# A graph layer on one core: silu by one ScalarE instruction, for two octs at a time, and another order in front

## The chip, the core and the metric

The kernel runs on one core of a Trainium2 chip. A core has TensorE (PE), VectorE (DVE), ScalarE (ACT), GpSimd (POOL) and SyncE (SP), each with its own queue of instructions, which it takes strictly in order; they meet at semaphores. The metric is the device time in microseconds. The kernel before takes 825.34 us, the median of three runs (822.86 to 827.72).

## The reference

12,500 nodes with 128 features and 400,000 edges, sorted by destination. Cut to what matters:

```python
rbf = exp(-(dist[:, None] - centers) ** 2 / (2 * width ** 2))      # 50 centers
cut = 0.5 * (cos(pi * dist / 10) + 1) * (dist <= 10)
W   = (silu(rbf @ fw1 + fb1) @ fw2 + fb2) * cut[:, None]
agg = segment_sum((h[src] @ pw + pb) * W, dst)
y   = h + (silu(agg @ mw1 + mb1) @ mw2 + mb2)
out = layernorm(h + y)
```

`dist` is `edge_weight`. Edges longer than the cutoff add nothing, and the kernel drops them: 141 quads of 512 edges are left to compute.

## The kernel before, in words

**Chunks and packing.** The edges are read in 7 chunks. `pack(c)` (a Python generator that emits some instructions at each step) squeezes the dropped edges out of a chunk on VectorE, scatters the lines that are left to `packed` in DRAM, reads them back (`pair`), and stores the lengths to `near_d`. It then makes `srci` (the source indices, for GpSimd's gathers), `base` and `dl` (where a message goes) and `cut`. `cut` needs a sine on ScalarE. Turning a row of these into places on partitions costs a transpose on TensorE each (L527) and a copy on VectorE (L529). Chunk 0 holds quads 0 to 6, chunk 1 quads 7 to 25, chunk 2 starts at quad 26.

**Projection.** `proj = h @ pw + pb` is computed for all nodes, in 25 tiles of up to four blocks of 128 rows: load, `turn` (transposes, and a copy to `xT` on ScalarE), `project` (matmuls, a copy to `hp` on ScalarE, a store by SP).

**Gathers.** `fetch(q)` is four indirect DMAs on GpSimd (L643), 128 rows each, into one of 8 quad buffers; from quad 24 on there are only four, because `own` takes the other four for messages and one-hot matrices. Quads 0 to 7 are gathered from `x` itself, so that they need not wait for `proj`; `multiply(q)` applies `pw` to them afterwards. From quad 8 on the gathers read `proj`.

**Filter.** Two quads make an oct. For each oct: `radials` has SP load the lengths, broadcast (`d`); `basis` is a square and an exp on ScalarE (L678, L679); `first` is the product with `fw1` into `ph`, of which there is one buffer (L688). `tanh` on ScalarE (L694) and `silu` on VectorE (L701) make s = (1 + tanh(ph / 2)) * ph, which is twice silu; `fw2_h`, half of `fw2` (L1035), makes up for it. `second(q)` is the product with that for one quad (L710, L713).

**Message and sum.** `message(q)` multiplies the filter with the gathered rows on VectorE (L720). `place(q)` makes the one-hot matrix times `cut` (L729), `sum_up(q)` multiplies the two on TensorE (L745), and `add` adds the result into `aggT` (L768). `nodes` does the second network and the layer norm for rows that are finished, among the quads; `finish` does the last ones.

**Order.** The order is written out by hand (`manual_schedule`): each engine gets its instructions in the order in which the Python code emits them. `clock`, `pool`, `tensor`, `awake` and `there_at` are the author's estimates of time; they decide only where pieces of `pack`, gathers and multiplications are emitted. `pack_until(us)` emits packing up to such a time. `ahead(k)` starts the filter in the last four tiles. After the projection `pack_until(math.inf)` emits all that is left of chunks 0 and 1 before message 0. The main loop then does, for quad q: packing, gathers for later quads, tanh, first and basis for later octs (every second quad), message q, second(q + 2), sum, place(q + 1), adds, silu.

**Tables.** ScalarE holds one set of activation functions at a time. Where the next function isn't in it, the built program has a table load, which stands in the profile as ACT_TABLE_LOAD with the line of that function.

Of the kernel before, what the change touches and what calls it, by code (L numbers as in the profile page):

```python
# [10 lines left out]
F32 = mybir.dt.float32  # L11
BF16 = mybir.dt.bfloat16
I32 = mybir.dt.int32
AF = mybir.ActivationFunctionType
OP = mybir.AluOpType
# [4 lines left out]
P = 128  # L20
# [6 lines left out]
QE = QT * P  # L27
# [11 lines left out]
NQ = QB[-1]  # L39
# [18 lines left out]
def kernel(  # L58
# [37 lines left out]
    nc = tc.nc  # L96
# [44 lines left out]
    def load_rows(c):  # L141

        raw[c] = []
        for name, ap, dt in (("r_d", edge_weight, I32), ("r_dst", dst, I32), ("r_src", src, I32)):
            t = work.tile([P, R_MAX], dt, name=name, bufs=2)[:, :ROWS[c]]
            v = ap[P * sum(ROWS[:c]):P * sum(ROWS[:c + 1])].rearrange("(r l) -> r l", r=P)
            nc.sync.dma_start(t, v if ap is not edge_weight else v.bitcast(I32))
            raw[c].append(t)
# [211 lines left out]
    def pack(c):  # L360
# [110 lines left out]
        else:  # L471
            awake[0] = 0.0
            if c > 1:
# [4 lines left out]
        pair = work.tile([64, 3, 512], I32, name="pair", bufs=1)  # L478
        dma.dma_start(pair[:np_], packed[:, p0 * 512:(p0 + np_) * 512]
                          .rearrange("s (p w) -> p s w", w=512))  # L480
        awake[c] = max(awake[c], clock[0]) + (7.5 if c == 1 else 3.5)
        yield 0

        def paired(dt, name):
# [116 lines left out]
    def project(t0):  # L601
        r = rows(t0)
        b = bank()
        h = b.rearrange("p (k f) -> p k f", k=4)
        rows_times(h, xT_of.pop(t0), pw_sb, bias_b["pb"], r)
        hp = work.tile([P, 4, H], F32, name="hp", bufs=3)
        for a, c, m in alike(r):
            nc.scalar.copy(hp[:m, a:a + c], h[:m, a:a + c])
        free.append(b)
        node_dma(t0, hp, proj, True)  # L610
# [37 lines left out]
    def quads(o):  # L648

        return [q for q in (2 * o, 2 * o + 1) if q < NQ]  # L650
# [20 lines left out]
    def chunk_of(q):  # L671
        return max(c for c in range(NC_) if QB[c] <= q)

    def basis(o):
        d, n = d_of.pop(o)
        u = n * 64
        rbf = work.tile([P, QE], F32, name="rbf")
        nc.scalar.activation(rbf[:u], d[:u], AF.Square, bias=rbf_bias[:u], scale=rbf_scale[:u])  # L678
        nc.scalar.activation(rbf[:u], rbf[:u], AF.Exp, scale=-1.0 / (2.0 * width * width))  # L679
        rbf_of[o] = rbf, n  # L680

    def first(o):

        rbf, n = rbf_of.pop(o)
        ph = ps.tile([P, 2, QE], F32, name="ph", bufs=1)
        for h in range(n):
            p0 = h * 64
            nc.tensor.matmul(ph[:, h, :], w1_sb[p0:p0 + KR], rbf[p0:p0 + KR], start=True, stop=True)  # L688
        ph_of[o] = ph, n

    def tanh(o):
        ph, n = ph_of[o]
        t = work.tile([P, 2, QE], F32, name="t", bufs=1)
        nc.scalar.activation(t[:, :n], ph[:, :n], AF.Tanh, scale=0.5)  # L694
        t_of[o] = t

    def silu(o):

        ph, n = ph_of.pop(o)
        s = work.tile([P, 2, QE], F32, name="s")  # L700
        nc.vector.scalar_tensor_tensor(s[:, :n], t_of.pop(o)[:, :n], 1.0, ph[:, :n],  # L701
                                       op0=OP.add, op1=OP.mult)
        for h in range(n):
            s_of[2 * o + h] = s[:, h]

    def second(q):

        s = s_of.pop(q)
        pu = bank()
        nc.tensor.matmul(pu, ones_b[:, :P], bias_b["fb2"].rearrange("k j f -> k (j f)"), start=True,  # L710
                         stop=False)
        for j in range(QT):
            nc.tensor.matmul(pu[:, j * H:(j + 1) * H], s[:, j * P:(j + 1) * P], fw2_h,  # L713
                             start=False, stop=(j == QT - 1))
        pu_of[q] = pu

# [7 lines left out]
    def place(q):  # L724

        hot = own(q, "hot", 1)
        for j in range(QT):
            at = 2 * q + j // 2, slice(j % 2, j % 2 + 1)
            nc.vector.tensor_scalar(hot[:, j, :], iota_n[:, :W], dl[:, at[0], at[1]],  # L729
                                    cut[:, at[0], at[1]], op0=OP.is_equal, op1=OP.mult)  # L730
        hot_of[q] = hot

    def windows(q):

        return 1 if chunk_of(q) < WIDE_C else 2
# [224 lines left out]
    def pack_until(us, among=2):  # L960

        while clock[0] < us and todo and todo[0] < among:
            have = [c for c in todo[:2] if c < among]
            c = next((c for c in have if awake[c] <= clock[0]), None)
            if c is None:
                clock[0] = min([us] + [awake[c] for c in have])
            else:
                go_on(c)
# [19 lines left out]

    def ahead(k):

        if k < 3:
            basis(k)
        if 0 < k:
            if k < 3:
                first(k - 1)
            if 1 < k:
                tanh(k - 2)
                silu(k - 2)
                clock[0] += 1.2

    for k, t0 in enumerate(tiles):
        if k + AHEAD_X < len(tiles):
            load_x(tiles[k + AHEAD_X])
        if loads and k >= 4 and k % 2 == 0:
            nc.sync.dma_start(*loads.pop(0))
        if k == 12:
            clear_packed(1, nc.sync)
        if k in (16, 19, 22):
            if k > 16:
                take_off()  # L1010
                clock[0] += 0.3
            take_off = part_of("fb2", fb2_f, (k - 16) // 3, False)
        if k == 23:
            load_rows(2)
        project(t0)
        clear(1, CLEARED)
        if k + 2 < len(tiles):
            turn(tiles[k + 2])
        tensor += 1.95
        pack_until(tensor)  # L1020
        fetches(tensor, FROM_X)
        while times[0] < fetched[0] and there_at[times[0]] <= tensor:
            multiply(times[0])
            times[0] += 1
            tensor += 1.9
            pack_until(tensor)
            fetches(tensor, FROM_X)
        if k in (17, 20, 23):
            radials((k - 14) // 3)
        if k >= len(tiles) - 4:  # L1030
            ahead(k - len(tiles) + 4)
    pack_until(math.inf)
    assert not loads and todo[0] == 2
    fw2_h = keep.tile([H, H], F32, name="fw2_h")
    nc.vector.tensor_scalar(fw2_h, fw2_sb, 0.5, None, op0=OP.mult)  # L1035
    fetches(clock[0], FROM_X)
    for q in (0, 1):
        second(q)
    first(2)
    place(0)  # L1040


    total, counted = None, []
    for q in range(NQ):
        while todo and todo[0] <= chunk_of(min(q + 3, NQ - 1)):
            go_on(todo[0])
        nodes(q)
        most[0] = min(NQ, max(min(q + GOT, sum(LATER)), q + LATER[1]))
        fetches(clock[0], most[0])
        fetches(math.inf, min(NQ, q + AHEAD + 1))  # L1050
        assert fetched[0] > min(NQ - 1, q + AHEAD)
        multiplies(q + 2)
        if q >= CLEAR_Q:
            clear()
        if loads_later and q >= 8:
            nc.sync.dma_start(*loads_later.pop(0))
        radials(q // 2 + 5)
        if q % 2 and q + 3 < NQ:
            tanh((q + 3) // 2)
        if q % 2 == 0 and 0 < q < NQ - 4:  # L1060
            first(q // 2 + 2)
        if q % 2 and q + 5 < NQ:
            basis((q + 5) // 2)
        msg = message(q)
        if q + 2 < NQ:
            second(q + 2)
        sum_up(q, msg)
        now = range(added(q), added(q + 1))
        for k in now:
            base_of(k, (0,))  # L1070
        if q + 1 < NQ:
            place(q + 1)
        for k in now:
            base_of(k, (1,))
            add(k)
        if q % 2 and q + 3 < NQ:
            silu((q + 3) // 2)
        clock[0] = max(clock[0], there_at[q])
        summed[q] = clock[0] + 0.7
        clock[0] += (3.1 if q % 2 else 1.9) + 0.3 * (windows(q) - 1)  # L1080
        if q == 1:
            clear_packed(2, nc.sync)
        if q + 1 < NQ:
            pack_until(max(there_at[q + 1], clock[0] + PACK_US), NC_)
        if NODES - 8 <= q < NODES - 2:
            part_of(*(("mb1", mb1_f) if q < NODES - 5 else ("mb2", mb2_f)), (q - NODES + 8) % 3)
        elif q == NODES - 2:
            late["mw2"] = mw2_h = keep.tile([H, H], F32, name="mw2_h")
            nc.vector.tensor_scalar(mw2_h, mw2_sb, 0.5, None, op0=OP.mult)
        if not todo and not counted:  # L1090
            counted.append(q)
            count()
        elif counted and total is None:
            total = nc.values_load(bad_i[0:1, 0:1], min_val=0, max_val=2 * E)
# [6 lines left out]
    with tc.If(total > 0):  # L1101
        nc.vector.memset(aggT, 0.0)
        def again(e0, seen):
# [21 lines left out]
            radial(-1, [edge_weight[ds(e0, QE)].rearrange("(o e) -> o e", o=1)])  # L1125
            basis(-1)
            first(-1)
            tanh(-1)
            silu(-1)
            second(-2)  # L1130
            u = own(0, "msg", 0)
# [51 lines left out]
```

## Time and profile before

| | |
|---|---|
| median of 3 runs | 825.34 us |
| profiled execution | 823.01 us |
| its span | 821.2 us |
| PE, DVE, ACT, POOL busy | 599.3, 662.6, 301.3, 571.8 us |
| tanh (L694) | 71 x 1015 ns |
| product for silu (L701) | 71 x 1207 ns |
| square and exp (L678, L679) | 71 x 806 and 71 x 630 ns |
| table loads | 15 x 1283 ns |
| gathers from `proj` | 532 x 990 ns, from 96.0 us on |
| mean granted clock | 0.856 |

Busy times are those of the span. In a row of a group of instructions come the line, the engine, the operation, what is written from what, and the count; then busy time, the mean time of one in ns, and the idle time just before them with what ended most of it ("issue": nothing that the profile shows). In a timeline row come the start, the duration and the same names, and in brackets the idle time before it and what it waited for. Idle time of an engine that sets nothing costs nothing. In such rows `fw_h` and `fw_sb` stand for `fw2_h` and `fw2_sb`.

### The profile page before, as it was taken

To read this page: it belongs to the slowest core of one execution; us is meant where nothing else is said; L and a number is where in the kernel's file an instruction comes from. 1 tells how busy PE (TensorE), PEld (TensorE's weight loads), DVE (VectorE), ACT (ScalarE), POOL (GpSimd) and SP (SyncE) were. 2 spreads that over 40 slices of the span, in tenths; PEclk is the share of its full clock that TensorE was granted. 3 is DMA by queue.
4 is the path that set the end of the run, shared out by engine and by line. 5 is a ranking of instruction groups with operands and counts; after the bars stand their busy time and mean duration, and the time that the engine had idled before them with its cause. 6 is when DMAs were issued, how large, how long until landed. Compare 5 with 4: busy or idle time off the path is not lost.

```text
span 821.2 us, 11643 instructions
## 1 busy us (share of the span) xinstructions
PE 599.3 (73%) x3492; PEld 463.6 (56%) x3492; DVE 662.6 (81%) x1857; ACT 301.3 (37%) x475; POOL 571.8 (70%) x585
## 2 busy tenths in 40 slices
PE   6874688777787676677768787878776786788661
PEld 6763566556565464565546466655554664666541
DVE  8852699999999788888998879888676766877774
ACT  7556343324334251223332333534331622251511
POOL 1474477777777777777777777777777777777740
PEclk9997699989978888687887887998999888999976
DMA  8984623243234223322242333543532543362221
GB/s 234 304 223 142 176 84 94 62 124 108 83 101 109 70 76 99 92 89 86 60 136 79 91 99 90 137 125 91 155 93 65 159 116 88 94 158 70 84 83 48
DMA packets 88189, 91.86 MB, mean 112 GB/s; under 512 B 13864, under 2 KB 67832, under 8 KB 88120
## 3 DMA queue, kind: packets, MB, share of 16 engines
q1 hardware_dynamic: 69320, 52.77, 21.9%
q0 software_dynamic: 18544, 38.17, 17.2%
q8 instruction: 29, 0.48, 0.2%
q14 instruction: 40, 0.33, 0.1%
q10 hardware_dynamic: 256, 0.11, 0.1%
HBM read 75.29 MB, written 15.71 MB: 111 GB/s over the span
## 4 chain that ended last, share of the span: by engine, by line
DVE 31%; DMA 21%; POOL 18%; issue 15%; PE 9%; DVEq 3%; ACT 2%; SPq 0%; POOLq 0%; ACTq 0%
DMA quad<-proj,srci 19%; POOL quad L643 18%; DVE hot L729 5%; DVE s L701 4%; DVE quad L729 3%; DVE aggT L768 3%; PE bank L277 3%; DVE msg L720 2%; DVEq L754 2%; PE sums L745 2%; DVE quad L720 1%; DMA x<-in_x_dram 1%; DVE st L808 1%; PE bank L713 1%; DVE r_d L438 1%
## 5 line engine op out<-in xcount | busy, mean ns | idle before, releaser
L643 POOL DMA_INDIRECT quad<-proj,srci x532 | 526.9, 990 | 171.7 <-issue 119.1
L713 PEld LDWEIGHTS bank<-fw_h,s 128*128 128x128 f32 x1128 | 177.9, 225 | 15.3 <-issue 7.5
L713 PE MATMUL bank<-fw_h,s 128*128 128x128 f32 x1128 | 177.5, 309 | 0.0
L688 PE MATMUL ph<-rbf,w_sb 51*128 51x512 f32 x282 | 98.0, 768 | 76.6 <-DVE s L701 60.1
L745 PE MATMUL sums<-hot,msg 128*128 128x128 f32 x696 | 111.3, 311 | 39.8 <-DVE msg L720 39.6
L694 ACT ACTIVATE t<-ph 128x1024 f32<-128x1024 f32 (+1 forms) x71 | 72.1, 1015 | 177.0 <-PE ph L688 173.4
L745 PEld LDWEIGHTS sums<-hot,msg 128*128 128x128 f32 x696 | 99.8, 221 | 47.1 <-DVE msg L720 46.7
L729 DVE TENSOR_SCALAR hot<-iota_n,dl,cut 128x128 f32<-128x128 f32 x348 | 97.7, 355 | 3.6 <-issue 1.0
L701 DVE SCALAR_TENSOR_TENSOR s<-t,ph 128x1024 f32<-128x1024 f32 (+1 forms) x71 | 85.7, 1207 | 16.9 <-ACT t L694 16.8
L720 DVE TENSOR_TENSOR msg<-bank,quad 128x512 f32<-128x512 f32 x87 | 59.4, 683 | 44.6 <-DMA quad<-proj,srci 39.9
L745 PE MATMUL sums<-quad,quad 128*128 128x128 f32 x432 | 68.4, 309 | 32.2 <-DVE quad L720 32.1
L745 PEld LDWEIGHTS sums<-quad,quad 128*128 128x128 f32 x432 | 61.6, 220 | 36.7 <-DVE quad L720 36.5
L688 PEld LDWEIGHTS ph<-rbf,w_sb 51*128 51x128 f32 x282 | 26.3, 214 | 98.2 <-issue 70.0
L768 DVE TENSOR_TENSOR aggT<-aggT,sums 128x128 f32 x212 | 60.6, 286 | 18.2 <-PE sums L745 7.2
L782 ACT ACTIVATE zt<-bank 128x512 f32<-128x512 f32 (+1 forms) x25 | 14.6, 587 | 165.2 <-PE bank L780 165.2
L710 PE MATMUL bank<-fb_b,ones_b 96*128 96x512 bf16 x141 | 61.6, 437 | 4.1 <-DVE msg L720 1.6
L729 DVE TENSOR_SCALAR quad<-iota_n,dl,cut 128x128 f32<-128x128 f32 x216 | 60.8, 350 | 2.3 <-issue 0.5
L720 DVE TENSOR_TENSOR quad<-bank,quad 128x512 f32<-128x512 f32 x54 | 37.1, 686 | 28.3 <-DMA quad<-proj,srci 28.1
L678 ACT ACTIVATE rbf<-d,rbf_bias,rbf_scale 128x512 f32<-128x512 f32 (+1 forms) x71 | 57.2, 806 | 5.1 <-DMA d<-near_d 5.0
L710 PEld LDWEIGHTS <-ones_b 96*128 96x128 bf16 x141 | 14.5, 103 | 68.7 <-issue 68.0
L847 ACT ACTIVATE x<-x,by,rs 128x128 f32<-128x128 f32 x91 | 36.9, 480 | 39.6 <-DVE by L817 39.6
L643 POOL DMA_INDIRECT quad<-in_x_dram,srci x32 | 33.1, 1033 | 20.2 <-DVE srci L529 10.0
(172 smaller groups left out, 746.2 us busy)
## 6 DMA issues: line engine op xcount, KB each, us to landing
d<-near_d SPq DMA_DIRECT2D x141, 128.0 KB
x<-in_x_dram SPq DMA_DIRECT2D x48, 256.0 KB
quad<-proj,srci POOLq DMA_INDIRECT x532
proj<-hp SPq DMA_DIRECT2D x24, 256.0 KB
out_dram<-x SPq DMA_DIRECT2D x24, 256.0 KB
packed<-zero_i SPq DMA_DIRECT2D x6, 188.0 KB
pair<-packed SPq DMA_DIRECT2D x3, 264.0 KB
r_d<-in_edge_weight_dram SPq DMA_DIRECT2D x3, 256.0 KB
```

Of the source, the lines that this page charges most:

```text
L643: nc.gpsimd.indirect_dma_start(out=got[:, j, :], out_offset=None, in_=proj if table is None else table, in_offset=bass.IndirectOffsetOnAxi ...
L678: nc.scalar.activation(rbf[:u], d[:u], AF.Square, bias=rbf_bias[:u], scale=rbf_scale[:u])
L688: nc.tensor.matmul(ph[:, h, :], w1_sb[p0:p0 + KR], rbf[p0:p0 + KR], start=True, stop=True)
L694: nc.scalar.activation(t[:, :n], ph[:, :n], AF.Tanh, scale=0.5)
L701: nc.vector.scalar_tensor_tensor(s[:, :n], t_of.pop(o)[:, :n], 1.0, ph[:, :n], op0=OP.add, op1=OP.mult)
L710: nc.tensor.matmul(pu, ones_b[:, :P], bias_b["fb2"].rearrange("k j f -> k (j f)"), start=True, stop=False)
L713: nc.tensor.matmul(pu[:, j * H:(j + 1) * H], s[:, j * P:(j + 1) * P], fw2_h, start=False, stop=(j == QT - 1))
L720: nc.vector.tensor_mul(msg, pu.rearrange("p (j f) -> p j f", j=QT), got_of.pop(q))
L729: nc.vector.tensor_scalar(hot[:, j, :], iota_n[:, :W], dl[:, at[0], at[1]], cut[:, at[0], at[1]], op0=OP.is_equal, op1=OP.mult)
L745: nc.tensor.matmul(pa[:, k * W:(k + 1) * W], msg[:, j, :], hot[:, j, :], start=(j % n == 0), stop=(j % n == n - 1))
L768: nc.vector.tensor_add(to, to, pa[:, k * W:(k + 1) * W])
L847: nc.scalar.activation(y[:m, k, :], y[:m, k, :], AF.Identity, bias=by[:m, k:k + 1], scale=rs[:m, k:k + 1])
```

## The change

`tanh` and the product become one activation, `Silu`, which reads `ph` and writes s; s has three buffers, and `fw2` is used as it is. In the main loop the filter goes by groups of four quads, that is two octs: at the fourth quad of a group the bases of two octs are computed, at the first and second quad of the next group `first` and `silu` of one oct each. `second` comes before `first` in each step.

In front: `ahead` does two bases and two silus; only quads 0 to 3 are multiplied among the tiles; chunk 2 is read at tile 17 instead of 23, and its packing may start among the tiles; after the projection only as much of chunk 1 is emitted as its indices need, and the rest of it comes among the first quads. The estimates of time differ too (a tile 2.25, a multiplication 2.1, a quad 2.2), and one clearing of `packed` moves from quad 1 to quad 0.

```diff
-        awake[c] = max(awake[c], clock[0]) + (7.5 if c == 1 else 3.5)
+        awake[c] = max(awake[c], clock[0]) + (10.5 if c == 1 else 3.5)
...
     def basis(o):
+        if o not in d_of:
+            for q in quads(o):
+                while chunk_of(q) not in stored:
+                    go_on(todo[0])
+            radials(o + 1)
...
-    def tanh(o):
-        ph, n = ph_of[o]
-        t = work.tile([P, 2, QE], F32, name="t", bufs=1)
-        nc.scalar.activation(t[:, :n], ph[:, :n], AF.Tanh, scale=0.5)
-        t_of[o] = t
-
     def silu(o):
-
         ph, n = ph_of.pop(o)
-        s = work.tile([P, 2, QE], F32, name="s")
-        nc.vector.scalar_tensor_tensor(s[:, :n], t_of.pop(o)[:, :n], 1.0, ph[:, :n],
-                                       op0=OP.add, op1=OP.mult)
+        s = work.tile([P, 2, QE], F32, name="s", bufs=3)
+        nc.scalar.activation(s[:, :n], ph[:, :n], AF.Silu)
...
-        if k < 3:
+        if k < 2:
             basis(k)
-        if 0 < k:
-            if k < 3:
-                first(k - 1)
-            if 1 < k:
-                tanh(k - 2)
-                silu(k - 2)
-                clock[0] += 1.2
+        if k > 1:
+            first(k - 2)
+            silu(k - 2)
...
-        if k == 23:
+        if k == 17:
             load_rows(2)
+            awake[2] = tensor + 10.0
...
-        tensor += 1.95
-        pack_until(tensor)
+        tensor += 2.25
+        among = 2 if k < 17 else 3
+        pack_until(tensor, among)
         fetches(tensor, FROM_X)
-        while times[0] < fetched[0] and there_at[times[0]] <= tensor:
+        while times[0] < min(fetched[0], 4) and there_at[times[0]] <= tensor:
...
-    pack_until(math.inf)
-    assert not loads and todo[0] == 2
-    fw2_h = keep.tile([H, H], F32, name="fw2_h")
-    nc.vector.tensor_scalar(fw2_h, fw2_sb, 0.5, None, op0=OP.mult)
+    while known[0] < QB[2]:
+        go_on(todo[0])
+    assert not loads
...
     for q in (0, 1):
         second(q)
-    first(2)
+    basis(2)
+    basis(3)
     place(0)
+
+    def octs(q):
+
+        return q // 4 * 2 + 2 + q % 4
...
-        if q % 2 and q + 3 < NQ:
-            tanh((q + 3) // 2)
-        if q % 2 == 0 and 0 < q < NQ - 4:
-            first(q // 2 + 2)
-        if q % 2 and q + 5 < NQ:
-            basis((q + 5) // 2)
         msg = message(q)
         if q + 2 < NQ:
             second(q + 2)
+        if q % 4 < 2 and 2 * octs(q) < NQ:
+            first(octs(q))
+            silu(octs(q))
+        if q % 4 == 3:
+            for o in (q // 4 * 2 + 4, q // 4 * 2 + 5):
+                if 2 * o < NQ:
+                    basis(o)
...
-        if q % 2 and q + 3 < NQ:
-            silu((q + 3) // 2)
...
-        clock[0] += (3.1 if q % 2 else 1.9) + 0.3 * (windows(q) - 1)
-        if q == 1:
+        clock[0] += 2.2 + 0.3 * (windows(q) - 1)
+        if q == 0:
             clear_packed(2, nc.sync)
```

More of the change, by code (lines that the diff above doesn't have):

```diff
@@ L712, in second @@
         for j in range(QT):
-            nc.tensor.matmul(pu[:, j * H:(j + 1) * H], s[:, j * P:(j + 1) * P], fw2_h,
+            nc.tensor.matmul(pu[:, j * H:(j + 1) * H], s[:, j * P:(j + 1) * P], fw2_sb,
                              start=False, stop=(j == QT - 1))
@@ L1018 @@
             turn(tiles[k + 2])
-        tensor += 1.95
-        pack_until(tensor)
+        tensor += 2.25
+        among = 2 if k < 17 else 3
+        pack_until(tensor, among)
         fetches(tensor, FROM_X)
-        while times[0] < fetched[0] and there_at[times[0]] <= tensor:
+        while times[0] < min(fetched[0], 4) and there_at[times[0]] <= tensor:
             multiply(times[0])
             times[0] += 1
-            tensor += 1.9
-            pack_until(tensor)
+            tensor += 2.1
+            pack_until(tensor, among)
             fetches(tensor, FROM_X)
@@ L1127, in again @@
             first(-1)
-            tanh(-1)
             silu(-1)
```

## The prediction, made before the changed kernel ran

> **What bounds the kernel now.** I read the table of engines first and the idle time of the busiest engines second. VectorE has the most busy time, yet the row that matters is GpSimd's gathers:
>
> ```profile
> span 821.2 us, 11643 instructions
> ...
> PE 599.3 (73%) x3492; PEld 463.6 (56%) x3492; DVE 662.6 (81%) x1857; ACT 301.3 (37%) x475; POOL 571.8 (70%) x585
> ...
> L643 POOL DMA_INDIRECT quad<-proj,srci x532 | 526.9, 990 | 171.7 <-issue 119.1
> ```
>
> 532 gathers cost 990 ns each, and in front of each one lie about 0.30 us of issue: 532 x 0.30 = 160 of the 171.7 us idle. So of the 171.7 us only some 12 are real waits. Four gathers make a quad: about 5.2 us a quad, 695.4 us from the first gather out of `proj` (96.03) to the end of the last (791.41). In this stretch GpSimd never stands still. The span is three pieces: 96.0 us of front, 695.4 us of gathers, 29.8 us of tail.
>
> The table by stage says the same: GpSimd runs 46 to 48 instructions in every 60 us, whether VectorE is nearly full (130 to 240 us) or not (600 to 660):
>
> ```profile
> 130.00:240.00 110.00, 81.62 (x492) 65.43 (x491) 106.93 (x272) 36.45 (x48) 84.43 (x84) 0.89 0.31 91
> 240.00:300.00 60.00, 43.01 (x226) 32.35 (x226) 50.71 (x128) 20.57 (x30) 46.26 (x46) 0.78 0.34 94
> 600.00:660.00 60.00, 44.33 (x269) 34.33 (x267) 43.21 (x127) 21.84 (x37) 45.54 (x48) 0.91 0.40 110
> ```
>
> (Columns after the stretch: PE, PEld, DVE, ACT, POOL, clock, DMA share, GB/s.) The real waits stand in the timeline of GpSimd's front:
>
> ```profile
> 70.57 0.94 POOL L643 DMA_INDIRECT quad<-in_x_dram,srci  x1 [0.31 <-issue]
> 81.48 0.94 POOL L643 DMA_INDIRECT quad<-in_x_dram,srci  x1 [9.97 <-DVE srci L529]
> ...
> 96.03 0.94 POOL L643 DMA_INDIRECT quad<-proj,srci  x1 [9.86 <-DVE msg L720]
> ```
>
> Two holes of 9.9 us: quad 7 waits for the indices of chunk 1, quad 8 for message 0. VectorE's timeline shows what both stand behind:
>
> ```profile
> 79.84 1.22 DVE L701 SCALAR_TENSOR_TENSOR s<-t,ph 128x1024 f32<-128x1024 f32 x1 [11.45 <-ACT t L694]
> 80.98 0.23 DVE L529 CAST srci<-bank 128x76 int32<-128x76 f32 x1
> 85.94 1.22 DVE L701 SCALAR_TENSOR_TENSOR s<-t,ph 128x1024 f32<-128x1024 f32 x1 [4.72 <-ACT t L694]
> ...
> 92.21 0.22 DVE L1035 TENSOR_SCALAR fw_h<-fw_sb 128x128 f32<-128x128 f32 x1
> 92.34 1.11 DVE L729 TENSOR_SCALAR hot<-iota_n,dl,cut 128x128 f32<-128x128 f32 x4
> 94.59 0.69 DVE L720 TENSOR_TENSOR msg<-bank,quad 128x512 f32<-128x512 f32 x1 [1.14 <-PE bank L713]
> ```
>
> The product of silu waits for tanh, and the finished indices of chunk 1 wait behind it in VectorE's order; then the whole rest of chunk 1 (87.08 to 92.2) and `fw_h` come before message 0.
>
> **The change part by part.**
>
> *Silu leaves VectorE.* 71 x 1207 ns = 85.7 us go. By the reading above this is worth nothing between 96 and 770 us, since GpSimd sets the pace and was not waiting; gathers late in the kernel, with the product still running, take 45.54/48 = 0.95 us, close to the median 0.944, so it was not slowing them either. What it buys there is margin. The gather of quad 28 reuses the buffer of quad 24; it starts at 202.76, and message 24 ends at 201.75, so VectorE is 1 us from holding GpSimd up. Between messages 0 and 24 VectorE loses 12 products (14.5 us), loses the first five steps of chunk 2 (2.6 us, now ahead of message 0) and gains the second half of chunk 1 (3 us). The margin there becomes about 13 us. That matters because GpSimd's start moves forward by the gain below, and VectorE, nearly full, must follow.
>
> *ScalarE.* Tanh (71 x 1015 ns) becomes a silu of the same shape; the trace has none, and I take tanh's row. Bounds: 0.8 us (the square of half that width costs 806 ns with pointer operands) and 2 us. Exp and silu need different tables. The changed program holds 78 table loads where 15 ran, 63 more. The row is
>
> ```profile
> 66.44 1.28 ACT L679 ACT_TABLE_LOAD   x1
> 67.73 0.63 ACT L679 ACTIVATE rbf<-rbf 128x512 f32<-128x512 f32 x1
> ```
>
> so 63 x 1.28 = 81 us, and ScalarE goes from 301 to 382 us of some 812. Here the Trainium skill speaks against the change: "ScalarE: Activation LUTs", section "What ACT_TABLE_LOAD costs", puts a switch at about 2.66 us, the load and a drain, and advises to batch by table set. By it the 63 loads cost 168 us, and ScalarE is at 469. The trace shows no drain: exp starts 10 ns after the load ends. I take 1.28. Either way a group of four quads (20.9 us) holds two loads, two bases (2 x 1.44) and two silus: 7.5 us by the row, 10.2 by the page, with the nodes' work (some 2 us) on top. ScalarE's slack hides it. If that cover went, it would show in TensorE's second product, which now has two to three quads, 10 us or more, between silu and use; before it had one quad. TensorE also waited 60.1 us for the product, with one `ph` buffer; that wait moves to ScalarE's silu one quad earlier, and nobody on the path waits for it.
>
> *The order in front.* This is where the time moves. On TensorE the multiplications of quads 0 to 3 now come two tiles earlier and 4 to 7 after the loop. (1) TensorE waits for landings: the last gather of quad 1 is issued at 44.08 and lands at 48.1, as in the trace; quad 2 follows at 52.2. After quad 2's product (54.7) eight tiles remain, 17 to 24, where five did. (2) Chunk 0's rest 1.3 us, tiles 17 and 18 at 1.55 each (the period in the dense stretch from 24 to 30 us): 59.2. Then TensorE meets chunk 0's cutoff: load 1.28, sine and square 0.82, VectorE 0.41, some latency: 62.6. Quad 3, 2.5 us: 65.1. Tiles 19 to 22: 71.3. (3) ScalarE then sets the pace, from 70.4 on: basis 0 with a load 2.7, a part of the bias 0.9, copies 1.2, basis 1 1.4, a copy 0.6, load 1.28, silu 1.02, last copies 0.8: 80.3. The last store of `proj` needs 0.8 to issue and an estimated 2 to land (the gathers in the trace take 2.4): 83. (4) Meanwhile TensorE turns chunk 1's indices after tile 24 (71), so quad 7 is gathered from 72 and the first hole closes: VectorE no longer stands behind tanh. (5) Message 0 needs silu 0 (79.5), the next `ph` (1.1 to 2.0), second(0) (1.5 to 2.6), the message 0.69, and 0.75 from its end to the gather: 83.5 to 85.5. TensorE's granted clock was 0.50 to 0.67 between 70 and 100 us, which is why I keep two values. (6) Quad 10 waits for message 2, which now stands behind chunk 1's cutoff on VectorE; that needs ScalarE to get through bases 2 and 3, two loads and silu 2 (7 us), behind `d` of oct 3, which SP can issue only after the last stores of `proj`. I get 92 to 98 for message 2, against a need of 94 to 96: a stall of nothing to 3 us. On SP the loads of chunks 2 and 3 (1.55 MB) come before the last stores; their buffers are long free, so they cost issue slots, some 3 us that the DMA share of 0.55 there hides.
>
> Taken together the stream of gathers starts, in effect, at 86 (82 to 91) in place of 96.0: 10 us less.
>
> *Tail.* From 775 us VectorE is busy without a gap up to message 140, with two products in the chain (1.21 and 0.68). Message 140 starts 3.9 us after the last gather's issue ends; elsewhere the least is 1.6. So 1.9 us can go; I take 1.5. The `zt` load at the end (1.28) also goes, but its wait was ScalarE's own.
>
> **Sum.** 823.0 (the profiled execution; 821.2 of it is span) - 10.0 - 1.5 = 811.5. That execution was 2.3 under the median of the runs, so: 814.
>
> **The rivals.**
>
> *Front gain eaten* (0.16): steps 3 to 6 each at their slow end, quad 8 at 88 and a stall of 3 at quad 10: start 91, 5 gained, tail nothing: 820. For it: ScalarE is a serial chain there, with table loads. Against it: VectorE's 16 us of waits for tanh go in any case.
>
> *Front gain larger* (0.11): TensorE at full clock, busier than before in 70 to 90, and `proj` landing sooner: start 81, tail 1.9: 808.
>
> *Silu becomes the wait* (0.12, slower): with four gather buffers, gather q needs message q-4, with about 13 us of margin in most quads and 8 in those with node work. If ScalarE's group (bases, loads, silus, node activations, all in one order) delivers s later than that, each group of four loses what is beyond the margin. It decides from about 8 us late; 1 us beyond it in each of 28 groups after quad 28 is 28 us, less 11: 842. For it: 63 more loads in an engine whose order also holds waits of 10 us for the normalization. Against: 7.5 to 10 us of work in 20.9, and earlier calls of silu.
>
> *No effect* (0.03): the front is held by something not shown, 825.
>
> **How the numbers follow.** The likeliest case has 0.58 and 814, with 809 to 819 as its own range. What tells from no change is about 0.5%, or 4 us: below 821.2 counts as faster. Likeliest and larger gain are faster, and of the eaten gain 0.10: 0.79. Same: 0.06 of it and the no-effect case: 0.09. Slower: 0.12. The range reaches from 806 to 825; it leaves out the slower rival and a little below.
>
> **What would show it.** Right: the first gather from `proj` near 86, quad 7 near 72; 690 to 697 us from there to the end of the last gather, with issue as the releaser throughout; about 78 table loads of 1.28; VectorE near 577 us busy; silu at tanh's duration. Wrong: the first gather from `proj` after 92; gathers waiting for msg in the stage with four buffers; TensorE waiting for s on ScalarE in every group; a load followed by a drain.

## The result, and the profile after

The changed kernel takes 815.96 us (median of 12 runs, 814.69 to 822.16) where the kernel before takes 825.92 (12 runs, 822.86 to 831.55): a ratio of 0.9884, 95% interval 0.9863 to 0.9904. A later set on another chip gave 817.56 against 825.80, 0.9899 (0.9869 to 0.9928). The forecast was 814. In the first three sets of experiments the chips gave every kernel, the one before too, medians of 1036 to 1133 us, so those ratios are read only against the kernel before on the same chip.

The time of the median is right, but two of the three terms behind it are not, so that the nearness of the number is luck; this is the lesson of the case. In two profiled executions of the changed kernel (the second is the run after_again_b), against the one of before:

| us | before | predicted | after | after, second |
|---|---|---|---|---|
| first gather from `proj` | 96.03 | 86 | 91.19 | 91.84 |
| from there to the end of the last gather | 695.4 | 695 | 694.3 | 693.6 |
| from there to the end of the span | 29.8 | 28.3 | 31.8 | 31.6 |
| span | 821.2 | | 817.3 | 817.0 |
| time of the profiled execution | 823.01 | 811.5 | 819.14 | 818.73 |

The head of the page after, and GpSimd's row in it:

```profile
span 817.3 us, 11550 instructions
...
PE 604.2 (74%) x3492; PEld 475.7 (58%) x3492; DVE 587.5 (72%) x1785; ACT 381.1 (47%) x536; POOL 569.8 (70%) x585
...
L643 POOL DMA_INDIRECT quad<-proj,srci x532 | 524.9, 987 | 169.6 <-issue 131.7
```

VectorE is 75 us less busy, and the 532 gathers with the issue in front of them take what they took: 524.9 + 169.6 us where it was 526.9 + 171.7. The stretches that were shown of before, after the change (after the stretch: PE, PEld, DVE, ACT, POOL, clock, DMA share, GB/s):

```profile
130.00:240.00 110.00, 83.15 (x516) 65.15 (x517) 99.73 (x272) 52.93 (x62) 84.73 (x82) 0.91 0.35 95
240.00:300.00 60.00, 44.97 (x223) 34.10 (x222) 48.21 (x126) 25.22 (x34) 46.28 (x46) 0.72 0.30 77
600.00:660.00 60.00, 44.72 (x253) 33.02 (x253) 36.88 (x122) 29.83 (x43) 45.37 (x49) 0.88 0.42 110
```

GpSimd runs 46 instructions in the 60 us from 240, as before, while VectorE went from 50.7 to 48.2 and ScalarE from 20.6 to 25.2. What a freed VectorE and a loaded ScalarE are worth there is read from the POOL column: nothing. The groups of the new silu and of its table loads:

```profile
L699 ACT ACTIVATE s<-ph 128x1024 f32<-128x1024 f32 (+1 forms) x71 | 72.3, 1018 | 197.9 <-PE ph L693 197.8
L684 ACT ACT_TABLE_LOAD x36 | 46.2, 1283 | 0.6
L699 ACT ACT_TABLE_LOAD x36 | 46.2, 1283 | 0.6
```

Silu costs what tanh did (1018 ns against 1015). The loads cost 1283 ns each, and ScalarE still stands idle 197.8 us for `ph`. GpSimd's two holes in front, in the timeline:

```profile
78.75 0.94 POOL L643 DMA_INDIRECT quad<-in_x_dram,srci  x1 [6.74 <-DVE part L541]
...
91.19 1.09 POOL L643 DMA_INDIRECT quad<-proj,srci  x1 [7.76 <-DMA d<-near_d]
92.59 0.94 POOL L643 DMA_INDIRECT quad<-proj,srci  x1 [0.30 <-issue]
```

They shrank from 9.97 and 9.86 us to 6.74 and 7.76 (8.04 and 7.00 in the second profile). The releasers named are the last by the time stamps, not the causes: quad 7 waits for `srci`, quad 8 for message 0, which ends at 90.92.

### The profile page after: what moved, and what is told of

Its sections match the earlier page's. It is cut to its first block, busy times and chain, and to the rows that moved or that the text cites. A ratio compares the mean times of both kernels' runs of the same rounds, so it can differ in the third digit from the quotient of the medians.

```text
span 817.3 us, 11550 instructions
## 1 busy us (share of the span) xinstructions
PE 604.2 (74%) x3492; PEld 475.7 (58%) x3492; DVE 587.5 (72%) x1785; ACT 381.1 (47%) x536; POOL 569.8 (70%) x585
## 4 chain that ended last, share of the span: by engine, by line
DVE 24%; POOL 20%; DMA 20%; issue 16%; PE 14%; ACT 3%; DVEq 2%; SPq 0%; POOLq 0%; ACTq 0%
POOL quad L643 20%; DMA quad<-proj,srci 18%; DVE hot L726 4%; PE sums L742 4%; PE bank L277 3%; DVE aggT L765 3%; DVE quad L726 2%; PE bank L710 2%; DVE msg L717 2%; DVEq L751 2%; PE ph L693 2%; DVE quad L717 1%; DVE r_d L438 1%; DVE nodes L429 1%; PE bank L595 1%
## 5 line engine op out<-in xcount | busy, mean ns | idle before, releaser
L643 POOL DMA_INDIRECT quad<-proj,srci x532 | 524.9, 987 | 169.6 <-issue 131.7
L710 PEld LDWEIGHTS bank<-fw_sb,s 128*128 128x128 f32 x1128 | 175.2, 222 | 37.1 <-issue 28.8
L710 PE MATMUL bank<-fw_sb,s 128*128 128x128 f32 x1128 | 173.5, 304 | 0.0
L699 ACT ACTIVATE s<-ph 128x1024 f32<-128x1024 f32 (+1 forms) x71 | 72.3, 1018 | 197.9 <-PE ph L693 197.8
L742 PEld LDWEIGHTS sums<-hot,msg 128*128 128x128 f32 x696 | 92.3, 206 | 115.4 <-DVE msg L717 84.8
L742 PE MATMUL sums<-quad,quad 128*128 128x128 f32 x432 | 79.3, 342 | 67.8 <-DVE quad L717 67.6
L742 PEld LDWEIGHTS sums<-quad,quad 128*128 128x128 f32 x432 | 70.2, 247 | 74.3 <-DVE quad L717 74.3
L693 PE MATMUL ph<-rbf,w_sb 51*128 51x512 f32 x282 | 89.5, 711 | 1.5 <-ACT s L699 1.4
L277 PEld LDWEIGHTS bank<-pw_sb,xT 128*128 128x128 f32 x260 | 40.0, 222 | 11.3 <-issue 5.1
L684 ACT ACT_TABLE_LOAD x36 | 46.2, 1283 | 0.6
L699 ACT ACT_TABLE_LOAD x36 | 46.2, 1283 | 0.6
L684 ACT ACTIVATE rbf<-rbf 128x512 f32<-128x512 f32 (+1 forms) x71 | 44.7, 630 | 1.5
```

The lines of the kernel that those rows point to most:

```text
L277: nc.tensor.matmul(to[:m, k, :], lT[:, k * P:k * P + m], w, start=False, stop=(k == a + c - 1))
L643: nc.gpsimd.indirect_dma_start(out=got[:, j, :], out_offset=None, in_=proj if table is None else table, in_offset=bass.IndirectOffsetOnAxi ...
L699: nc.scalar.activation(s[:, :n], ph[:, :n], AF.Silu)
L742: nc.tensor.matmul(pa[:, k * W:(k + 1) * W], msg[:, j, :], hot[:, j, :], start=(j % n == 0), stop=(j % n == n - 1))
```

## The experiments

**The changed kernel and the kernel before, again** (no edit).

> The changed kernel as it is, for a second profile and beside the other kernels of this study. All theories: 816 us, 10 less than before. By the front theory (A: the gain is that the gathers from proj start earlier) the first gather from proj starts near 91 in the profile of before's 96, the gathers take 694 to 696 us again, and what is left over of the 10 us beyond 5 is how far two single profiles scatter: the tail, 31.8 in the first profile against 29.8 before, should come back to 29 to 30.

> The kernel before as it is, for a second profile. All theories: 823 to 828; first gather from proj at 96, plus or minus 1, gathers 695 us, tail 29 to 31.

> The changed kernel as it is, on the same chip as early_filter_c, so that the two can be told apart. Where TensorE stands still as in the runs so far: 0.985 to 0.991 of before. Where it doesn't: 814 to 818 us, first gather from proj at 89 to 92, gathers 694 to 696, tail 29 to 32.

The first two ran on a chip where nothing kept to its pace: 0.9883 (0.9843 to 0.9922) of before at 1055.68 us, and profiles of 1050.6 (before) and 1052.6 us. They can't test the 91 and 96 us. after_again_b ran where the kernel before takes 825.80: 817.56 us, the first gather from `proj` at 91.84, 693.6 us of gathers. The expected front and middle came back. The tail did not: 31.6 us, not 29 to 30, so the 2 us that the tail has lost are no scatter of one profile.

That second profile shows where the front, which gave half of what was forecast, was late. VectorE's timeline:

```profile
70.81 0.15 DVE L374 CAST first<-r_dst 128x1 f32<-128x1 int32 x1 [6.97 <-DMA r_dst<-in_dst_dram]
...
73.22 0.68 DVE L488 TENSOR_TENSOR pair<-pair 38x512 int32<-38x512 int32 x1
...
75.03 0.28 DVE L506 TENSOR_SCALAR f_src<-part 38x256 f32<-38x256 int32 x1
...
79.63 0.24 DVE L529 CAST srci<-bank 128x76 int32<-128x76 f32 x1 [4.12 <-PE bank L527]
...
90.87 0.69 DVE L717 TENSOR_TENSOR msg<-bank,quad 128x512 f32<-128x512 f32 x1 [5.28 <-ACT rbf L683]
```

The first step of chunk 2 stands ahead of chunk 1's `pair` in VectorE's order, and waits 7 us for rows that SP asked for at 59.9 us and that came at 70.8. In the kernel before, chunk 1's `pair` ran at 66.26. This wait did not set the start, though: the indices (`f_src`) were ready at 75.3 and were turned only at 79.2, and ahead of message 0 VectorE stood idle for 5.28 us. TensorE's timeline of the same profile:

```profile
74.16 0.63 PE L595 MATMUL bank<-ident,x 128*128 128x128 f32 x4 [3.19 <-DMA x<-in_x_dram]
...
79.21 0.32 PE L527 MATMUL bank<-ident,f_src 38*128 38x38 f32 x2
```

A tile waits for its own load as well, and the turning of chunk 1's indices comes at 79.2 behind the last tiles (predicted 71). The stretches from 50 or 60 to 80 us, before:

```profile
50.00:60.00 10.00, 8.36 (x71) 7.54 (x70) 3.79 (x17) 5.70 (x11) 7.68 (x8) 1.00 0.65 185
60.00:70.00 10.00, 5.84 (x37) 3.95 (x35) 2.82 (x8) 8.44 (x14) 7.66 (x8) 0.96 0.54 159
70.00:80.00 10.00, 4.42 (x24) 3.67 (x22) 0.16 (x1) 5.60 (x9) 1.21 (x2) 0.67 0.56 174
```

and in the second profile after:

```profile
60.00:70.00 10.00, 6.65 (x30) 5.54 (x31) 0.86 (x3) 5.08 (x10) 7.56 (x9) 0.66 0.80 226
70.00:80.00 10.00, 6.80 (x43) 6.25 (x42) 4.90 (x13) 5.14 (x8) 1.80 (x2) 0.83 0.96 289
```

and in the first:

```profile
50.00:60.00 10.00, 8.83 (x46) 7.92 (x47) 3.68 (x18) 3.74 (x7) 7.56 (x9) 0.67 0.33 95
60.00:70.00 10.00, 6.40 (x33) 5.29 (x33) 1.65 (x7) 4.94 (x8) 7.56 (x9) 0.67 0.82 234
```

The DMA engines went from 0.54 and 0.56 busy to 0.80 and 0.96. The loads of chunks 2 and 3 now fall on those of `x` and the stores of `proj`. That the crowding made `x` and the rows late fits these numbers, but no run moved the loads back alone. In the first profile it isn't what made TensorE late: from 67.1 to 78.3 TensorE waits for no load there, and turns the indices at 77.83. Its granted clock was 0.67 from 50 to 70, where it had been 1.00 and 0.96 in the kernel before.

**ScalarE's work taken out of the end of the front.** To the changed kernel:

```diff
-        if k in (17, 20, 23):
-            radials((k - 14) // 3)
-        if k >= len(tiles) - 4:
-            ahead(k - len(tiles) + 4)
+        if k in (12, 13, 23):
+            radials(3 if k == 23 else k - 11)
+        if 14 <= k < 18:
+            ahead(k - 14)
```

> The changed kernel with the two bases and two silus of the front at tiles 14 to 17 instead of 21 to 24, where ScalarE stands idle for the gathers of quads 1 and 2, and the lengths loaded at tiles 12 and 13; two table loads fewer. A: ScalarE's chain ahead of the last store of proj (9.1 us in the changed kernel) becomes 3, quad 7 still comes at 78 to 79, and the first gather from proj starts at 84 to 86 instead of 91.2; 809 to 811. Rival (the start is not what sets the end: message 24 is only 0.5 us ahead of the gather of quad 28, and VectorE sets the pace to there): gathers from proj take 699 to 701 us, 814 to 816.

> The kernel of early_filter once more, hoping for a chip on which the kernel before takes 825 us and not 1060. A (the gain is where the gathers from proj start): first gather from proj at 84 to 86 where the changed kernel had 91.2, gathers 694 to 697, 809 to 811, that is 0.980 to 0.983 of before. Rival (VectorE sets the pace as far as quad 28): gathers 699 to 701, 814 to 816, 0.988. Should TensorE again stand still without a wait: 0.985 to 0.990, and nothing told apart.

> The kernel of early_filter beside the changed kernel on one chip. A (the start of the gathers sets the end): where GpSimd sets the pace, 5 to 7 us less than the changed kernel, first gather from proj at 84 to 86. Where TensorE stands still: 0 to 4 us less, since ScalarE has 6 us less to do ahead of the last store of proj but the gathers wait for messages later in any case. Rival (VectorE sets the pace to quad 28): the same time as the changed kernel, within 2 us, in both cases.

Beside the changed kernel on one chip: 814.57 against 817.56 us (0.9847, 0.9809 to 0.9884, against 0.9899, 0.9869 to 0.9928, of before; the intervals still touch). On the chips of the earlier sets 0.9864 (0.9823 to 0.9906) and 0.9841 (0.9783 to 0.9899). It is the fastest kernel of the study, and faster than before, with all three intervals below 1; that it is faster than the changed one is likely, not shown. That ScalarE's chain holds the start, it does show. The chain in the changed kernel, second profile:

```profile
77.65 0.81 ACT L683 ACTIVATE rbf<-d,rbf_bias,rbf_scale 128x512 f32<-128x512 f32 x1
78.48 1.28 ACT L684 ACT_TABLE_LOAD   x1
...
84.08 1.28 ACT L699 ACT_TABLE_LOAD   x1
85.38 1.02 ACT L699 ACTIVATE s<-ph 128x1024 f32<-128x1024 f32 x1
86.30 0.42 ACT L608 COPY hp<-bank 128x128 f32<-128x128 f32 x2
```

With bases, loads and silus gone from it, the last copy of `hp` starts at 79.75 and not at 86.30, and message 0 (VectorE's row) and GpSimd's timeline of early_filter_c are

```profile
81.59 0.69 DVE L717 TENSOR_TENSOR msg<-bank,quad 128x512 f32<-128x512 f32 x1 [1.25 <-issue]
```

```profile
77.21 0.94 POOL L643 DMA_INDIRECT quad<-in_x_dram,srci  x1 [5.69 <-DVE part L541]
...
85.93 0.94 POOL L643 DMA_INDIRECT quad<-proj,srci  x1 [4.03 <-DMA d<-near_d]
...
118.41 0.94 POOL L643 DMA_INDIRECT quad<-proj,srci  x1 [1.95 <-DVE msg L717]
...
129.21 0.94 POOL L643 DMA_INDIRECT quad<-proj,srci  x1 [6.11 <-DVE msg L717]
```

The first gather from `proj` is at 85.93, inside the expected 84 to 86 and 5.9 us ahead of the changed kernel. So ScalarE's serial chain is what set that start. Message 0 is now done 3.65 us ahead of that gather; what is left for it to wait for is the last store of `proj`, which SP issued at 80.8, 5.1 us before (no row shows its landing). On the chips of the earlier sets the start did not move: 107.9 us in early_filter and 109.0 in early_filter_b, where after_again has 108.1. TensorE's tiles were late there, and the last copy of `hp` started at 103.2 and 104.4 against 102.9.

But in this execution the gathers then stand still for messages 6, 7 and 8, 9.2 us in three places (1.95, 6.11 and, near 136 us, 2.05, less the usual 0.30 each), and they take 702.7 us in all; the execution took 821.04, while four of the six took 811.2 to 816.7. VectorE's timeline at that place, and the stretches of 110 to 130 us:

```profile
106.65 0.69 DVE L717 TENSOR_TENSOR msg<-bank,quad 128x512 f32<-128x512 f32 x1 [0.47 <-ACT quad L618]
111.74 1.63 DVE L726 TENSOR_SCALAR hot<-iota_n,dl,cut 128x128 f32<-128x128 f32 x4 [4.39 <-PE sums L742]
...
117.45 0.69 DVE L717 TENSOR_TENSOR msg<-bank,quad 128x512 f32<-128x512 f32 x1 [1.76 <-ACT quad L618]
```

```profile
110.00:120.00 10.00, 8.65 (x36) 6.81 (x34) 4.38 (x10) 2.19 (x3) 6.23 (x8) 0.50 0.16 39
120.00:130.00 10.00, 8.65 (x33) 6.43 (x32) 3.28 (x9) 3.96 (x5) 3.28 (x4) 0.50 0.11 28
```

One quad takes 10.8 us there, at a granted clock of 0.50 (in the changed kernel 0.83 to 1.00 in these stretches). A quad of this stage holds a multiplication (of quads 4 to 7, which the change moved here from the tiles), a first, a second and a sum, each waiting for the one before through ScalarE or VectorE. The rival that VectorE sets the pace as far as quad 28 is wrong in its engine: VectorE is 33 to 44% busy there. In this execution something does take the start back, and it is TensorE's chain. That the clock is why it took so long is read from this one profile; it fits that the two longest of the six executions, 821.04 and 823.81 us, have the lowest mean clocks, 0.843 and 0.846, and the other four 0.853 to 0.863. The changed kernel has the same stage. There messages 6, 7 and 8 end 2.9, 1.7 and 1.9 us ahead of the gathers that need their buffers, where before it was 6.6, 8.4 and 8.5.

**One part alone: silu, in the order of before.** To the kernel before:

```diff
     def tanh(o):
-        ph, n = ph_of[o]
-        t = work.tile([P, 2, QE], F32, name="t", bufs=1)
-        nc.scalar.activation(t[:, :n], ph[:, :n], AF.Tanh, scale=0.5)
-        t_of[o] = t
+        ph, n = ph_of.pop(o)
+        s = work.tile([P, 2, QE], F32, name="s", bufs=3)
+        nc.scalar.activation(s[:, :n], ph[:, :n], AF.Silu)
+        for h in range(n):
+            s_of[2 * o + h] = s[:, h]
...
     def silu(o):
+        pass
...
-                             s[:, j * P:(j + 1) * P], fw2_h,
+                             s[:, j * P:(j + 1) * P], fw2_sb,
```

> The kernel before, in its own order, with tanh replaced by Silu (ScalarE writes s at tanh's place) and the product on VectorE and fw2_h gone: 142 or so table loads, one for each basis and one for each silu. A (the front sets the gain, the middle is paced by GpSimd): VectorE no longer stands behind tanh with the indices of chunk 1, so quad 7 comes at 72 to 75 instead of 81.5, and message 0 some 3 to 6 us earlier; 820 to 823, gathers 694 to 696 us. B (the 86 us that VectorE loses are the gain): all of it, 814 to 817, with gathers shorter than 690. C (table loads cost): slower than before, about 830, with TensorE waiting for s.

> The kernel of silu_only once more, on another chip (0.9947 of before where every kernel took 28% longer). A: gathers 694 to 696 us; the front 3 to 6 us shorter, since VectorE no longer waits for tanh ahead of chunk 1's indices; 820 to 823, about half of the change's gain. B: 814 to 817, with gathers below 690. C: 830, TensorE waiting for s behind 140 table loads.

> The kernel of silu_only once more, for the same reason. A: first gather from proj at 90 to 93 (VectorE no longer stands behind tanh ahead of the indices of chunk 1), gathers 694 to 696, 820 to 823, 0.994 to 0.997 of before. B (the 86 us of VectorE are the gain): gathers below 690, 814 to 817. C: 830 and over, TensorE waiting for s behind 140 table loads.

0.9947 (0.9910 to 0.9984), 0.9915 (0.9875 to 0.9954) and 0.9893 (0.9833 to 0.9953). All three lie below 1 with their intervals, so the 138 loads around basis and silu do not cost what the silu saves, and theory C falls. Here A and B can't be told apart: on these chips the gathers wait in some 45 places (42 in before_again), mostly for messages, so their pace is not GpSimd's, and a freed VectorE may count. The intervals overlap that of the whole change on such a chip (0.9883), so that what the order adds to silu can't be told there. The first gather from `proj` came at 121.6, 118.8 and 115.8 us where before_again has 122.1.

**The other part alone: the order, with tanh and the product.** To the changed kernel:

```diff
         if q % 4 < 2 and 2 * octs(q) < NQ:
             first(octs(q))
-            silu(octs(q))
+            tanh(octs(q))
...
             add(k)
+        if q % 4 < 2 and 2 * octs(q) < NQ:
+            silu(octs(q))
```

with `tanh`, the product on VectorE and `fw2_h` as before.

> The changed kernel's order with tanh and the product on VectorE put back (tanh where Silu stood, the product at the end of the step, fw2_h made before message 0): 15 table loads. A: the first gather from proj is 3 to 5 us earlier than before, at 91 to 93, since most of the reordering stays; but message 24 has 12 products ahead of it again, so that the gather of quad 28 waits some 2 to 6 us and takes the gain back: 820 to 826, gathers 696 to 702 us. B (VectorE's time): 825, nothing gained. C (silu is worth nothing, the order does it all): 816, gathers 694 to 696.

> The kernel of order_only once more, on another chip (where it ran first every kernel took 28% longer, and this one was 3.5% slower than before). A: the first gather from proj at 91 to 93, then gathers that wait in the stage of quads 26 to 40, since message 24 has 12 products ahead of it again: 820 to 828, gathers 697 to 705 us. B (VectorE's 86 us as such are the gain): 825, gathers 695, nothing lost. C (silu is worth nothing, the order does it all): 816. D (from the run on the slow chip: TensorE's and ScalarE's chain of first, tanh, product and second is now the wait, with one ph buffer that is held until the end of the step): 840 or more, with gathers waiting for messages in many quads.

1.0352 (1.0277 to 1.0428) and 1.0661 (1.0586 to 1.0736): slower than before, the second time as D had it. The start moved ahead of before (115.9 and 116.0 us against 122.1), and the gathers lost more: 952.6 and 964.0 us against 887.1. The waits of order_only_b (us in total, times, the longest):

```profile
DVE s L706 <- ACT t L699: 254.4, 46, 16.7
...
POOL quad L643 <- DVE msg L725: 155.2, 30, 9.9
```

and of before_again:

```profile
POOL quad L643 <- DVE msg L720: 87.4, 20, 9.9
...
DVE s L701 <- ACT t L694: 35.2, 8, 12.6
```

VectorE stands 254 us for tanh. In this order `first`, tanh and the product are of one step, and what is late on TensorE goes through ScalarE to VectorE and holds the next message. So the two parts do not add up: on these chips the order is a loss unless silu ends on ScalarE. Neither part was run alone where the kernel before takes 825 us; how the gain there divides between them is open.

**VectorE's time alone.** The changed kernel with an operation of the product's size that waits for nobody, at the end of each step that makes a silu:

```diff
+        if q % 4 < 2 and 2 * octs(q) < NQ:
+            nc.vector.scalar_tensor_tensor(pad, pad, 1.0, pad, op0=OP.add, op1=OP.mult)
```

> The changed kernel with a VectorE operation of the old product's size (128 x 1024, on a tile of its own, waiting for no other engine) put where the product stood, at the end of each step that makes a silu, 69 in all. It is work added, none left out. A: VectorE gets some 80 us busier, which costs the margin of quads 24 to 30 alone: 816 to 822, all of it between quads 24 and 34, nothing after quad 40. B (VectorE's time as such is the gain): 824 to 826, spread over the gathers. C (VectorE's time is worth nothing anywhere): 816, gathers 694.

```profile
L1080 DVE SCALAR_TENSOR_TENSOR pad<-pad 128x1024 f32<-128x1024 f32 x69 | 83.9, 1216 | 0.0
```

0.9943 (0.9902 to 0.9984) of before, with 83.9 us of work added. The changed kernel had 0.9883 (0.9843 to 0.9922) on another chip. The 84 us cost 0.6%, some 6 us, at intervals that overlap. Even this is not VectorE's time alone, since in this profile the gathers themselves are slower:

```profile
L643 POOL DMA_INDIRECT quad<-proj,srci x532 | 557.0, 1047 | 319.1 <-issue 149.3
```

In after_again they took 520.4 us, 978 ns each. One of them, and what VectorE does meanwhile:

```profile
371.85 1.73 POOL L643 DMA_INDIRECT quad<-proj,srci  x1 [0.30 <-issue]
```

```profile
371.55 1.22 DVE L1080 SCALAR_TENSOR_TENSOR pad<-pad 128x1024 f32<-128x1024 f32 x1
```

The 96 gathers that overlap a `pad` operation take 1404 ns on average, the other 436 take 968. In the kernel before, the 117 that overlap the product take 954 and the others 1001. So the product did not slow the gathers, as the prediction said, but its stand-in does. `pad` takes both operands from SBUF, while the product took `ph` from PSUM; whether that is the reason, no run shows.

The two runs of order_only, with as much work and the wait, lie 4.7 and 7.8% over the changed kernel's ratio. Of what order_only lost, the wait for tanh is the bulk and VectorE's time is little. The quads in which the 6 us lie can't be named, since those chips have waits everywhere.

## Why the prediction was right or wrong

**GpSimd sets the pace from `proj` to the end: right.** 695.4 us became 694.3 and 693.6; after the first gather from `proj` no gather waits longer than 0.6 us in front. The 1.1 to 1.8 us less are the gathers' own, 987 ns against 990, times 532.

**Silu off VectorE is worth nothing in the middle: right; the margin it buys: wrong.** The step said that message 24 would come about 13 us ahead of the gather of quad 28. It came 0.5 us ahead (198.69 against 199.20), in the second profile 3.2; before it was 1.0. The step counted VectorE's work and left out its waits and its order. In the first profile it stands 9.3 us for TensorE and ScalarE between 110 and 185 (3.70, 2.12 and 1.28 us at messages 6 and 7, 2.22 at 182), and packing comes ahead of messages: chunk 2 is scattered at 159.7 where it was 169.9. Message 24 is about as close to the gather as before. Busy time fell by 75 us, not by 85.7, in part because rows overlap: the product of 79.84 us in the kernel before is shown for 1.22 us, and the next instruction starts after 1.14.

**ScalarE: right.** Silu 1018 ns for a forecast of 1015, 76 loads where 78 were counted, 381.1 us busy for 382, and no load followed by a drain. Of the Trainium skill's 2.66 us a switch ("ScalarE: Activation LUTs", "What ACT_TABLE_LOAD costs") the trace has the load, 1283 ns, and not the drain; with both, the estimate was 469 us. (The page's advice to batch by table set stands in its section "Table sets: the hidden batching unit".) TensorE waited 1.4 us in the whole execution for a silu to free `ph`; before it was 60.1 for the product. The rival in which silu becomes the wait did not come.

**The order in front: the failed step.** Forecast 10 us, measured 4.8 and 4.2. Steps (3) and (5) have the right lengths: ScalarE's chain took 9.1 us where 9.9 were forecast, and from the first silu's end to the first gather from `proj` it was 5.1 and 5.4 where 4 to 6 were. What failed is when the chain starts: basis 0 at 77.3 and 77.65 and not at 70.4. This is step (2), which sized TensorE's work by a dense stretch of the kernel before (24 to 30 us, a granted clock of 1.00), at 1.55 us a tile and 2.5 us for quad 3, and put the end of tiles 19 to 22 at 71.3.

In the first profile chunk 0's cutoff was 4.5 us late, at 67.1 where 62.6 was forecast, and quad 3 took 3.9 us, with TensorE at a clock of 0.67 from 50 to 70; it waited for no load after that. In the second the cutoff was in time, at 63.0, quad 3 took 3.9 us again at a clock of 0.66, and then TensorE waited 3.2 us for `x`. So two executions were late by nearly the same amount in different ways. Why the clock was lower there than in the kernel before is open.

Two more terms were wrong. Step (6) had the cover "they cost issue slots, some 3 us that the DMA share of 0.55 there hides". The share was taken from the kernel before, and with the loads moved it was 0.80 and 0.96 in the second profile, in which `x` came late. Step (3) put 2 us for the last store of `proj` to land; in early_filter_c, with message 0 done, the gather starts 5.1 us after that store is issued.

Step (4) had quad 7 at 72; it was 78.75 and 80.14. TensorE turned the indices behind its late tiles, at 77.8 and 79.2, 2.6 and 3.9 us after VectorE had them ready. VectorE's own wait for `r_dst`, which the step left out, would have put quad 7 near 76 on its own (an estimate: ready at 75.2, and 0.9 us from the turning to the gather), but it is not on the path of quad 8. The stall at quad 10 did not come: message 2 is 2.3 and 1.7 us ahead.

**Tail: wrong in sign.** 1.5 us were to go, 1.8 to 2.0 came. Message 140 did start earlier after the last gather (3.7 and 3.5 us after its end against 3.9), so at most 0.4 us came of the product's absence. But from that start to the end it took 28.1 us in both profiles, where it was 25.9. That chain is the second network and the layer norm of the last rows, and its matmuls took longer. The same ones after (first profile), and before:

```profile
792.72 2.07 PE L777 MATMUL bank<-aggT,mw_sb 128*128 128x512 f32 x2 [0.28 <-DVE aggT L765]
```

```profile
798.84 1.55 PE L780 MATMUL bank<-aggT,mw_sb 128*128 128x512 f32 x2 [0.27 <-DVE aggT L768]
```

The granted clock is 0.65 and 0.63 from 785 to 800 in the two profiles after, 0.69 from 791 to 805 before. That the clock is the cause fits, and was not tested.

**The sum.** By its terms the forecast for the profiled execution was 811.5; it was 819.1 and 818.7. The rival "front gain eaten", start at 91 and nothing in the tail, describes the profiles better than the likeliest case. The median still fell by 10.0 and 8.2 us, since the profiled execution of before lies 2.9 us under the median of its 12 runs and those of the changed kernel lie 3.2 and 1.2 over theirs. The forecast added 2.3 us for that on both sides. So the median came within 2 us of the forecast by luck: the front and the tail, which were to give 11.5 us, gave 2.8 and 2.4, and what the executions without a profile gain beyond the 4 us of the two profiled ones is open. The mean clock does not tell it: of the 12 executions of the changed kernel the longest, 822.16 us, had 0.858 and the shortest, 814.69, 0.857. early_filter_c shows that one execution can lose 9 us in a stage of 20 us at a clock of 0.50, which would be enough; that this happened in the profiled ones is not shown, and in their profiles no gather waits so.

## What to carry to other kernels

A forecast of a serial front needs its first link right: here ScalarE's chain had about the length forecast, and began 7 us late. Do not take TensorE's pace for a stage from a stretch where it ran at full clock. When a load is moved earlier, take the DMA share of the place it goes to, with the load added, not of the place as it was; and look for the first instruction that uses it, in that engine's order, and for what stands behind it. A stage that one engine paces makes changes to the others free, but the front that feeds it is a serial chain, and work in it counts nearly in full: early_filter moved 6.5 us of bases, table loads and a silu to where ScalarE stood idle, and in early_filter_c the start came 5.9 us earlier. Two parts of a change need not add up, so run each alone, and look at what else a stand-in touches: `pad` was to cost VectorE's time, and slowed the gathers too.

## What the runs showed of the hardware

On three sets of runs TensorE started late where it had nothing to wait for. Its weight loads and matmuls near 312 us of before_again (PEld, then PE):

```profile
310.41 1.35 PEld L745 LDWEIGHTS sums<-hot,msg 128*128 128x128 f32 x6 [4.51 <-DVE msg L720]
311.99 0.29 PEld L745 LDWEIGHTS sums<-hot,msg 128*128 128x128 f32 x1 [0.23 <-issue]
313.42 0.29 PEld L745 LDWEIGHTS sums<-hot,msg 128*128 128x128 f32 x1 [1.14 <-issue]
```

```profile
312.72 0.37 PE L745 MATMUL sums<-hot,msg 128*128 128x128 f32 x1 [0.66 <-issue]
314.11 0.37 PE L745 MATMUL sums<-hot,msg 128*128 128x128 f32 x1 [1.02 <-issue]
```

Load and matmul take turns every 0.70 us, where the six ahead of them went at 0.21. In that profile 42 weight loads that wait for no semaphore started over 0.4 us late, in the first profile of before none; on VectorE there is one such start in either, on ScalarE and GpSimd none. The mean granted clock was 0.74 to 0.77 in these sets against 0.84 to 0.86. The transfers of instructions do not tell the two profiles apart (29 packets on their queue in either, 0.2% of the span); what the cause is, these profiles do not show.

Silu and the sine of the cutoff need no table load between them: with the silus ahead of chunk 0's sine, early_filter has 74 loads where the changed kernel has 76, and none stands between the two.
